# Ten loads moved from SyncE's DMA queue to GpSimd's: the residual for its turn, the output matrix and its bias

## The chip, the cores and the metric

The kernel runs on one core of one Trainium2 chip. Its time is the device time of one execution in microseconds (us); a lower time is better. A core has five engines that work side by side, each through its own list of instructions in order: PE (matrix multiplication), DVE (vector work), ACT (activation functions, copies), POOL (GpSimd) and SP (SyncE). A transfer between the large memory (HBM) and the on-chip memory is issued by one of the engines, as an instruction in its list, and then runs by itself on the core's 16 DMA engines. In this kernel SP does nothing but issue transfers (nearly all loads), and POOL issues nearly all stores. An issue instruction that must wait, for a buffer to be free or for data to be written, holds everything behind it in its engine's list.

## The reference, cut to what matters

Two layers of attention over a picture of 48 by 48 positions (N = 2304 tokens, 768 channels, 12 heads of 64), each on a group-normalised input, each added to the residual:

```
x = x + layer0(group_norm(x))      # qkv with a low-rank addition to q and v
x = x + layer1(group_norm(x))      # qkv with q scaled twice

layer(x):
    q, k, v = x @ qkv_w + qkv_b                    # 12 heads of 64
    s = q @ k.T * scale + rel_h[q, key row] + rel_w[q, key column]
    o = softmax(s) @ v
    return o @ proj_w + proj_b
```

All data is float32. The tables `rel_h` and `rel_w` depend on the query and on the row or the column of the key.

## The kernel before, in words

Each layer runs three stages: `project` (normalise, make k, v, q and the position terms, store them to HBM), attention (`attend_plain`), and `out_project` (the product with the output matrix, plus the residual).

**Attention.** The loop goes over six pairs of heads, and for each pair over five blocks of queries: four of 512 and one of 256. A block's 18 key tiles (`kt`) are done in two batches of nine. For a tile PE makes the scores of both heads (L954, `ps_sc`, three PSUM buffers), ACT takes their exponential (L981, `pt`), and DVE adds it to a running sum (L987, from the second tile of a block on). PE is always one batch of scores ahead of the products with v: in `catch_up` it runs, for the batch before, the products `ps_ov` and, for a block's second batch, first the denominators `ps_d` from the sum. DVE then takes their reciprocal (L1021) and multiplies (L1025), ACT adds the bias of v (L1026), and POOL stores the denominators' reciprocals (L1032, `f_rec`) and the block (L1030, `f_o`). At the end of a block's sum ACT and DVE split it in three bfloat16 parts (L996 to L999).

The exponentials are taken without subtracting the row's maximum; at the end `judge` looks at the stored reciprocals, and only if they are out of range is everything computed again by a slower way (`attend_shifted`). With these inputs that second run isn't taken, and all that follows is about the first.

**What SP loads in attention, in this order.** For each block, while the block before it is computed: two loads of q (L932) and 24 of the position terms (`rel`, L942 and L946). At the end of a pair, also the four loads of the next pair's keys (L899, `k`, two for each batch of tiles) and two of its values (L908, `v`). The keys have one set of buffers, so a load of keys waits until PE has used the last pair's keys of the same batch.

**What runs beside it.** After every block but the first, `next(beside, None)` runs one step of the generator `beside`. In layer 0 its steps are: load the output matrix's bias (`bt`, L1288, shown as `bproj`) and the output matrix (`w_all`, L1293, shown as `wproj`, 2304 KB), and then four additions on the matrix, one a step (L412). In layer 1, between the two loads, comes `turn`: for each of six pieces of the residual (`res`, channels by tokens, 1152 KB each, numbered 0 to 5) it loads the piece (L1223, `x_turned<-f_res`), adds the bias on ACT (L1226, six activations, three in each of two steps), transposes 32 by 32 blocks on DVE (L1231) and stores the piece by 24 small transfers issued by POOL (L1238, `f_res_tokens`, 48 KB each). All pieces, and then the output matrix, use the same single buffer (tag `"w"` in the pool `p3_w`, one buffer). So the load of the next piece, and the load of the matrix, can only be issued when the 24 stores of the piece before have been written.

**What sets the order.** A scheduler places the instructions of each engine ahead of time; `in_order` keeps those it names in the order in which the program gives them on their engine. Each queue has eight semaphores for its transfers, used in turn: an issue also waits for the transfer eight places before it in the same queue.

Of the kernel before, what the change touches and what calls it, by code (L numbers as in the profile page):

```python
# [18 lines left out]
P = 128  # L19
# [52 lines left out]
def compute(ctx: ExitStack, tc: tile.TileContext, x, layers, out, run, bad):  # L72


    nc = tc.nc
# [35 lines left out]
    def scratch(name, shape):  # L111
        name = f"{run}_{name}"
        return dram.tile(shape, F32, tag=name, name=name)
# [16 lines left out]
    with ExitStack() as hots:  # L130
# [4 lines left out]
        for i, (rows, pattern, shape) in enumerate(parts):  # L135
            t = hotp.tile([rows, *shape], F32, tag=f"h{i}", name=f"hot_{i}")
# [21 lines left out]
    def in_order(instruction):  # L158

        tc.keep_in_program_order(instruction)  # L160
# [4 lines left out]
    def load_transposed(xT, raw, res, weights, low_rank):  # L165


        with tc.tile_pool(name="ps_x", bufs=3, space=PSUM) as ps_x:
            loaded = [xT[b].rearrange("p t q -> p (t q)") for b in range(NQB)]
            loaded = [l.rearrange("p (j c) -> p j c", j=TPB) for l in loaded]  # L170
            for b in range(NQB):
                nc.sync.dma_start(loaded[b], x[ts(b, QB), :].rearrange("(j p) c -> p j c", p=P))
            weights.load(0)
            weights.begin()
            if not shifted:
                load_places()
            for b in range(NQB):
                if b == 2:
                    next(low_rank)
                for t in range(CT):  # L180
                    ps = ps_x.tile([P, QB], F32, tag="ps", name=f"psx_{b}_{t}")
                    for j in range(TPB):
                        in_order(nc.tensor.transpose(
                            ps[:, ts(j, P)], loaded[b][:, j, ts(t, P)], ident
                        ))
                    nc.scalar.copy(raw[b][:, t, :], ps)
                    nc.vector.bn_stats(stats[:, t, b, :], raw[b][:, t, :])

            weights.spread()
            for b in range(HB):  # L190
                for i in (b, b + HB):
                    in_order(nc.gpsimd.dma_start(res[i], raw[i]))

    def group_norm(xT, raw, gn, between, beside):


# [220 lines left out]
    def matrix_blocks(w, n):  # L417

        return {
            f"{j + 1}{i + 1}": w[:, i * HP : (i + 1) * HP, ts(j, n)]  # L420
            for i in range(2) for j in range(2)
        }
# [28 lines left out]
    def project(ly, li, xT, kv, weights, first, normalise):  # L451


        PARTS = range(1 if shifted else 2)
        PART = F32 if shifted else F32R
        qd, kd = (
            [[scratch(f"{x}{li}_{half}_{i}", [P, HP, N]) for i in PARTS] for half in range(2)]
            for x in "qk"
        )

        vd = scratch(f"v{li}", [N, C])
        rel_d = [
            [
                [scratch(f"r{li}_{a}_{half}_{i}", [2 * HG, HP, N]) for i in PARTS]
                for half in range(2)
            ]
            for a in range(2)
        ]
        project_kv(ly, li, xT, kv, weights, first, normalise, PARTS, PART, kd, vd)
        return qd, kd, vd, rel_d  # L470

    def third_of_k(weights, g):

        w, room = weights.take("k", g)
        s = room.rearrange("p (i t n) -> p i t n", i=3, t=HP)
        return sums_of_a(matrix_blocks(w, P), *(s[:, i] for i in range(3)))
# [739 lines left out]
    def turn(res, to, pool, bt):  # L1216


        for b in range(NQB):

            both = pool.tile([P, 2, CT, QB], F32, tag="w", name=f"x_turned_{b}")
            x, turned = both[:, 0], both[:, 1]
            in_order(nc.sync.dma_start(x, res[b]))  # L1223
            yield
            for t in range(CT):
                in_order(nc.scalar.activation(  # L1226
                    x[:, t], x[:, t], AF.Identity, bias=bt[:, t : t + 1]
                ))
                if t == HP - 1:
                    yield  # L1230
            in_order(nc.vector.transpose(  # L1231
                turned.rearrange("p t q -> p (t q)"), x.rearrange("p t q -> p (t q)")
            ))
            rows = to[ts(b, QB), :].rearrange("(f i) c -> i f c", i=32)
            for t in range(CT):
                for r in range(P // 32):
                    lo = t * P + r * 32
                    in_order(nc.gpsimd.dma_start(  # L1238
                        rows[:, :, lo : lo + 32],
                        turned[ts(r, 32), t].rearrange("p (f j) -> p f j", j=32),  # L1240
                    ))
# [19 lines left out]
    for li, ly in enumerate(layers):  # L1261
        last = li == len(layers) - 1
        with tc.tile_pool(name="p1_kv", bufs=1, **REUSE) as kv:
            raw = xT
            low_rank = weights.low_rank(kv)
            if li == 0:


                raw = [
                    kv.tile([P, 2, CT, QB], F32, tag=tag, name=f"raw_{tag}")  # L1270
                    for tag in ("t1", "t2", "vw")
                ]
                raw = [raw[b % HB][:, b // HB] for b in range(NQB)]
                load_transposed(xT, raw, residuals[0], weights, low_rank)
                first, k_steps = third_of_k(weights, 0)
            normalise = group_norm(xT, raw, gn, low_rank, k_steps)
            qd, kd, vd, rel_d = project(ly, li, xT, kv, weights, first, normalise)
        project_q(ly, li, xT, weights, qd, rel_d)
        es.close()
        od = [  # L1280
            scratch(f"o{li}_{lo}", [CT, P, min(OB, N - lo)]) for lo in range(0, N, OB)
        ]
        with tc.tile_pool(name="p3_w", bufs=1, **REUSE) as p3:
            bt = p3.tile([P, CT], F32, tag="bt", name="bproj")
            w = {}

            def beside(li=li, ly=ly, p3=p3, bt=bt, w=w):
                in_order(nc.sync.dma_start(bt, ly.proj_bt))  # L1288
                if li == 1:
                    yield from turn(residuals[1], res_tokens, p3, bt)  # L1290
                w_all = p3.tile([P, CT, C], F32, tag="w", name="wproj")
                s = p3.tile([P, 3, HP, HP * P], F32, tag="s", name="wproj_s")
                in_order(nc.sync.dma_start(w_all, ly.proj_w.rearrange("(t p) n -> p t n", p=P)))  # L1293
                factors, steps = sums_of_a(
                    matrix_blocks(w_all, HP * P), *(s[:, i] for i in range(3))
                )
                w.update(factors)
                yield
                yield from steps

            attend(li, qd, kd, vd, rel_d, od, beside())


            es = ExitStack()
            xT = None
            if last:
                p3_first = es.enter_context(
                    tc.tile_pool(name="p3_first", bufs=1, side="right", **REUSE)
                )

                y_2, y_1, *first_out, y_0 = (
                    p3_first.tile(shape, F32, tag=name, name=name)
                    for name, shape in (
                        ("y_1_2", [P, 2, C]), ("y_1_1", [P, 2, C]), ("oT_1_0", [P, CT, QB]),
                        ("oT_1_1", [P, CT, QB]), ("y_1_0", [P, 2, C]),
                    )
                )
                first_out += [y_0, y_1, y_2]
            else:
                xT, gn, weights = begin(1, es)  # L1320
                first_out = [xT[HB], xT[NQB - 1]]
            prepared = []

            def prepare(weights=weights):
                weights.begin()
                weights.spread()
                weights.load(0)
                prepared.extend(third_of_k(weights, 0))
                yield
                yield from prepared[1]  # L1330

            k_steps = prepare()
            out_project(
                li, od, w, bt, first_out, res_tokens if last else residuals[li], xT,
                None if last else residuals[li + 1], iter(()) if last else k_steps,
            )
            if not last:
                first, k_steps = prepared
# [56 lines left out]
```

## Time and profile before

| what | us |
|---|---|
| median of three runs | 3287.63 |
| lowest and highest run | 3285.56 and 3287.98 |
| the profiled execution's own time | 3286.01 |
| its span, from the first instruction to the last | 3284.0 |
| PE busy in the span | 3209.8 (98%) |
| DVE busy | 2111.7 (64%) |
| ACT busy | 1450.6 (44%) |
| POOL busy | 462.0 (14%) |
| granted clock of PE, mean over the span | 0.99 |
| attention of layer 0, first to last reciprocal (L1021) | 976.39 |
| attention of layer 1, the same | 1006.36 |

Of the profiled execution's 3286.01 us, 2.0 us lie outside its span. The numbers in the timeline are microseconds from the span's start. The two layers run the same attention on the same shapes, so the two last rows can be laid side by side, reciprocal by reciprocal: there are 30, one for each pair and block. The difference between two neighbouring starts is called a lap here. In the profile, "issue" is time in which an engine waited for nothing that the profile shows, SPq is SP's list of issues, and the granted clock of PE is 1.00 at full speed.

### The profile page before, as it was taken

The numbers are of one execution on the slowest core, as the hardware profiler recorded it, in microseconds if no ns is written. First come the engines' busy times: TensorE is split into PE (matmuls) and PEld (weight loads), VectorE is DVE, ScalarE is ACT, GpSimd is POOL, SyncE is SP. The second block draws the span as 40 slices with busy tenths as digits, with TensorE's granted clock in tenths as the row PEclk, the third lists the DMA queues.
The fourth block names the chain that finished last, engine by engine and source line by source line (L and its number), as shares of the span: only waits on it lengthen the run. The fifth ranks groups of instructions, "written<-read, shape, count | busy, mean of one in ns | idle before, by whom it ended". The sixth has DMA issues, their size and how long they took to land.

```text
span 3284.0 us, 50036 instructions
## 1 busy us (share of the span) xinstructions
PE 3209.8 (98%) x19600; PEld 1993.1 (61%) x19600; DVE 2111.7 (64%) x2281; ACT 1450.6 (44%) x1673; POOL 462.0 (14%) x845
## 2 busy tenths in 40 slices
PE   8999999999999999999989999998999989999998
PEld 5555666566656566656555566665665556656565
DVE  8432437777777777776774234676777767777764
ACT  3101336555555555553011024564665555555520
POOL 2144110000000000000012531102223200000000
PEclk9999999999999999999999999999999999999999
DMA  7333488353435262725234346756556463435251
GB/s 266 130 82 76 133 263 217 83 124 81 123 82 136 68 147 67 151 61 180 93 127 139 55 123 204 228 124 142 116 137 129 119 162 75 127 80 133 69 201 59
DMA packets 226148, 419.77 MB, mean 128 GB/s; under 512 B 43840, under 2 KB 111328, under 8 KB 222064
## 3 DMA queue, kind: packets, MB, share of 16 engines
q1 hardware_dynamic: 180432, 267.16, 32.5%
q0 software_dynamic: 45472, 149.32, 15.2%
q8 instruction: 158, 2.59, 0.4%
q14 instruction: 86, 0.70, 0.1%
HBM read 260.35 MB, written 155.97 MB: 127 GB/s over the span
## 4 chain that ended last, share of the span: by engine, by line
PE 89%; issue 3%; DVE 3%; DMA 2%; ACT 1%; POOL 1%; SPq 1%; DVEq 0%; POOLq 0%; ACTq 0%
PE ps_sc L954 34%; PE ps_ov L954 24%; PE ps_q L698 9%; PE ps_v L523 7%; PE psy L1186 7%; PE ps_k L523 4%; PE psr L637 1%; PE ps_d L954 1%; DVE sum L987 1%; PE psc L637 1%; DMA rel<-f_r 1%; DVE relw L392 1%; POOL f_k L567 1%; ACT pt L981 1%; ACT relw L391 0%
## 5 line engine op out<-in xcount | busy, mean ns | idle before, releaser
L987 DVE TENSOR_TENSOR sum<-sum,pt 128x1024 f32<-128x1024 f32 (+1 forms) x960 | 1070.9, 1116 | 187.4 <-ACT pt L981 96.7
L954 PE MATMUL ps_sc<-q,k 64*128 64x512 f32 (+1 forms) x8640 | 1087.1, 371 | 25.2 <-issue 11.8
L981 ACT ACTIVATE pt<-ps_sc 128x1024 f32<-128x1024 f32 (+1 forms) x1080 | 1010.3, 941 | 196.4 <-PE ps_sc L954 110.5
L954 PEld LDWEIGHTS ps_sc<-q,k 64*128 64x128 f32 x8640 | 781.7, 186 | 239.4 <-issue 69.0
L954 PE MATMUL ps_ov<-pt,v 128*64 128x512 f32 (+1 forms) x4320 | 857.7, 551 | 0.0
L954 PEld LDWEIGHTS ps_ov<-pt,v 128*64 128x64 f32 x4320 | 301.1, 137 | 497.6 <-issue 443.3
L954 PE MATMUL ps_sc<-rel,places 64*128 64x512 f32 (+1 forms) x2160 | 414.0, 371 | 1.6 <-DMA rel<-f_r 1.3
L698 PE MATMUL ps_q<-xT,w_q 128*128 128x384 f32 x864 | 285.3, 489 | 0.7 <-DVE v L587 0.7
L1032 POOL DMA_DIRECT2D f_rec<-rec x120 | 58.4, 491 | 1612.1 <-DVE rec L1021 1612.1
L1026 ACT ACTIVATE o<-o,v_bias 128x512 f32<-128x512 f32 (+1 forms) x60 | 40.9, 682 | 450.4 <-DVE o L1025 450.4
L954 PEld LDWEIGHTS ps_sc<-rel,places 64*128 64x128 f32 x2160 | 211.8, 185 | 33.7 <-DMA rel<-f_r 1.6
L698 PEld LDWEIGHTS ps_q<-xT,w_q 128*128 128x128 f32 x864 | 163.1, 191 | 110.3 <-issue 2.6
L1021 DVE RECIPROCAL rec<-ps_d 128x512 f32<-128x512 f32 (+1 forms) x60 | 181.8, 3030 | 2.5 <-PE ps_d L954 2.5
L987 DVE TENSOR_TENSOR sum<-pt 128x1024 f32<-128x1024 f32 (+1 forms) x60 | 67.0, 1117 | 146.5 <-ACT pt L981 146.5
L601 POOL DMA_DIRECT2D f_v<-v x288 | 137.3, 485 | 106.5 <-DVE v L587 94.8
L523 PE MATMUL ps_k<-xt,w_k 128*128 128x384 f32 x432 | 143.4, 487 | 3.6 <-DVE xt L427 2.6
L704 DVE TENSOR_SCALAR x_q<-ps_q,bt 128x384 f32<-128x384 f32 x72 | 44.3, 617 | 159.4 <-PE ps_q L698 159.4
L996 ACT CAST sum<-sum 128x1024 bf16<-128x1024 f32 (+1 forms) x60 | 57.6, 960 | 169.3 <-DVE sum L987 169.3
L523 PE MATMUL ps_k<-xT,w_k 128*128 128x384 f32 x324 | 115.7, 511 | 4.7 <-DVE xT L249 4.6
L523 PEld LDWEIGHTS ps_k<-xt,w_k 128*128 128x128 f32 x432 | 81.5, 190 | 63.0 <-PE ps_k L523 3.0
L999 DVE TENSOR_TENSOR sum<-sum,sum 128x1024 bf16<-128x1024 f32 (+1 forms) x60 | 67.1, 1119 | 61.6 <-ACT sum L998 61.6
L997 DVE TENSOR_TENSOR sum<-sum,sum 128x1024 f32<-128x1024 f32 (+1 forms) x60 | 67.1, 1118 | 61.6 <-ACT sum L996 61.6
(180 smaller groups left out, 2464.3 us busy)
## 6 DMA issues: line engine op xcount, KB each, us to landing
rel<-f_r SPq DMA_DIRECT2D x1152, 96.0 KB, 4.2
f_k<-xs POOLq DMA_DIRECT2D x72, 384.0 KB, 2.9
f_q<-xs_q POOLq DMA_DIRECT2D x48, 576.0 KB, 3.8
k<-f_k SPq DMA_DIRECT2D x48, 576.0 KB, 5.1
q<-f_q SPq DMA_DIRECT2D x96, 256.0 KB, 3.3
f_r<-relh POOLq DMA_DIRECT2D x48, 432.0 KB, 5.0
f_r<-relw POOLq DMA_DIRECT2D x8, 2592.0 KB, 18.0
f_v<-v POOLq DMA_DIRECT2D x288, 48.0 KB, 2.0
```

The costliest lines, as they stand in the source:

```text
L523: nc.tensor.matmul(ps, lhsT=x, rhs=y, start=(t == 0), stop=(t == HP - 1))
L601: nc.gpsimd.dma_start(vd[to : to + KG, :], v[ts(r, KG), k])
L637: nc.tensor.matmul(ps[:, i, :, :], lhsT=weights.tables[a][:, 2 * s : 2 * (s + HG)], rhs=lines_of(l0 + i), start=True, stop=True,)
L698: nc.tensor.matmul(ps, lhsT=w[:, t, ts(pr, P)], rhs=xT[b][:, t, :], start=(t == 0), stop=(t == CT - 1),)
L954: in_order(nc.tensor.matmul(*args, **kwargs))
L981: nc.scalar.activation(pt, ps[:, :, 0 : self.n], AF.Exp)
L987: nc.vector.tensor_add(self.sum, self.first if kt == 1 else self.sum, pt)
L997: nc.vector.tensor_sub(self.sum, self.sum, hi)
L999: nc.vector.tensor_sub(lo, self.sum, mid)
L1021: nc.vector.reciprocal(self.rec, ps)
L1032: nc.gpsimd.dma_start(recs[li][2 * self.pair + r : 2 * self.pair + r + 1, to], self.rec[r * HD : r * HD + 1, :],)
L1186: nc.tensor.matmul(ps, lhsT=x, rhs=y, start=(t == 0), stop=(t == HP - 1))
```

## The change

Three calls change their engine, from `nc.sync` (SP) to `nc.gpsimd` (POOL). On the run that is executed these are ten transfers: the bias of each layer (two), the output matrix of each layer (two), and the six pieces of the residual in layer 1. What is loaded, where to, and the buffers stay as they are.

```
@@ turn
-            in_order(nc.sync.dma_start(x, res[b]))
+            in_order(nc.gpsimd.dma_start(x, res[b]))
@@ beside
-                in_order(nc.sync.dma_start(bt, ly.proj_bt))
+                in_order(nc.gpsimd.dma_start(bt, ly.proj_bt))
                 if li == 1:
                     yield from turn(residuals[1], res_tokens, p3, bt)
                 w_all = p3.tile([P, CT, C], F32, tag="w", name="wproj")
                 s = p3.tile([P, 3, HP, HP * P], F32, tag="s", name="wproj_s")
-                in_order(nc.sync.dma_start(w_all, ly.proj_w.rearrange("(t p) n -> p t n", p=P)))
+                in_order(nc.gpsimd.dma_start(w_all, ly.proj_w.rearrange("(t p) n -> p t n", p=P)))
```

Because POOL keeps the calls named by `in_order` in the order of the program, each moved load stands in POOL's list behind the 24 stores that free its buffer. In that list the load of piece 1 comes behind a store of `o` and two of the reciprocals, those of pieces 2, 3 and 5 and of the output matrix behind the stores of one block as well, and that of piece 4 directly behind the 24 stores. The lists of PE, DVE and ACT are the same in both kernels on the run that is executed; SP's list lacks the ten loads, and in two places two loads of q stand three places later among the loads of `rel`.

## The prediction

> **What bounds the kernel now.** I read the page first: PE is busy for 98% of the span, so time can only be won where PE stands still or runs at a lower clock. The laps between the reciprocals (L1021) show where. Layer 1's 30 laps follow layer 0's within 0.1 us almost everywhere, and sum to 1006.36 - 976.39 = 29.97 us more. Two laps hold nearly all of it:
>
> ```profile
> 2254.99 3.35 DVE L1021 RECIPROCAL rec<-ps_d 128x512 f32<-128x512 f32 x1
> 2296.31 1.75 DVE L1021 RECIPROCAL rec<-ps_d 128x256 f32<-128x256 f32 x1
> ...
> 2609.85 3.35 DVE L1021 RECIPROCAL rec<-ps_d 128x512 f32<-128x512 f32 x1
> 2651.47 1.75 DVE L1021 RECIPROCAL rec<-ps_d 128x256 f32<-128x256 f32 x1
> ```
>
> These laps are 41.32 and 41.62 us; the same lap at an undisturbed end of a pair (2962.52 to 2990.98) is 28.46. The excesses are 12.9 and 13.2 us, 26 together. They lie at the ends of pairs 0 and 2 of layer 1; call them gap A and gap B. The timeline shows what PE waits for:
>
> ```profile
> 2243.24 0.30 SPq L946 DMA_DIRECT2D rel<-f_r  x1
> 2266.04 0.34 SPq L1223 DMA_DIRECT2D x_turned<-f_res  x1
> 2272.35 1.62 ACT L1226 ACTIVATE x_turned<-x_turned,bproj 128x384 f32<-128x384 f32 x3 [1.77 <-DMA x_turned<-f_res]
> 2275.08 2.51 SPq L899 DMA_DIRECT2D k<-f_k  x4
> 2280.81 1.22 PE L954 MATMUL ps_sc<-q,k 64*128 64x512 f32 x4 [11.19 <-DMA k<-f_k]
> ...
> 2622.12 0.40 SPq L1293 DMA_DIRECT2D wproj<-in_proj_w_dram  x1
> 2631.15 1.36 DVE L412 TENSOR_TENSOR wproj_s<-wproj 128x1152 f32<-128x1152 f32 x1 [4.99 <-DMA wproj<-in_proj_w_dram]
> 2631.68 1.91 SPq L899 DMA_DIRECT2D k<-f_k  x4
> ```
>
> SP issues nothing from 2243 to 2266, because the load of piece 1 waits for piece 0's stores. The next pair's keys stand behind it and go out at 2275; PE, done at 2269.6, waits for them until 2280.8. In gap B the matrix does the same (PE idle 2624.2 to 2636.0). SP's waits name the cause, and an undisturbed end of a pair shows keys issued in time:
>
> ```profile
> SPq L1223 <- DMA f_res_tokens<-x_turned: 109.9, 14, 21.4
> SPq L1293 <- DMA f_res_tokens<-x_turned: 21.4, 4, 17.0
> ...
> 2959.68 14.95 SPq L899 DMA_DIRECT2D k<-f_k  x4
> 2978.12 1.19 PE L954 MATMUL ps_sc<-q,k 64*128 64x512 f32 x8
> ```
>
> The windows show that a gap costs more than its length: PE's clock falls during it and is still at half when work returns (columns: us, busy of PE, PEld, DVE, ACT, POOL with counts, clock, DMA share, GB/s):
>
> ```profile
> 2270.00:2281.00 11.00, 0.19 (x2) 0.23 (x4) 0.69 (x1) 2.20 (x4) 0.00 (x0) 0.62 1.06 223
> 2283.00:2285.00 2.00, 2.00 (x14) 1.53 (x12) 0.00 (x0) 1.02 (x1) 0.00 (x0) 0.50 1.06 360
> 2285.00:2287.00 2.00, 2.00 (x16) 1.58 (x14) 0.00 (x0) 0.87 (x1) 0.00 (x0) 0.69 1.15 325
> ```
>
> Full clock for 24% of the first window means it fell about 3 us into the gap; 38% of the last puts its return at 2286.2. So 5.4 us ran at half clock, 2.7 us of lost work.
>
> **The change part by part.**
>
> *Off SP.* Ten issues go: 6 x 0.34, 2 x 0.43 and 2 x 0.36 us, 3.6 in all, plus 131 us of holding. The rest of SP's order matters only at gaps A and B; elsewhere PE was fully busy through 20 us holds, because loads run a block ahead. At A the keys' first half is free when PE has passed tile 8 of the last block (about 2251) and the second at about 2265.3; both go as at 2959 to 2975, in time. I take the wait for keys as gone at A and B.
>
> *On to POOL.* The six pieces have the shape of L1214's stores on POOL (0.53 us each); the matrices are nearest to L630's (0.72), the biases to L1032's (0.49). That is 5.6 us of POOL, which is busy 14% of the span. Queued behind a waiting load are `f_rec` and `f_o`; their buffers are double and needed again a block (18 to 37 us) later, while the load waits about 2 us for the last store to land. I cost that at nothing; were it longer than a block, DVE would stop at L1025.
>
> *Pieces 2 to 5.* They issue right after stores that POOL issues anyway, at 2339.0, 2414.0, 2476 and 2547.3, against 2338.8, 2412.0, 2475.7 and 2545.4 on SP. With 0.5 us of issue and 6.5 to land they arrive 5 to 8 us before their activations (2353.8, 2428.8, 2488.0, 2562.4). Piece 0 has 50 us. Cost nothing; the cover is those 5 us at piece 4. Layer 0's loads have over 40 us before L412.
>
> *Piece 1, gap A.* The stores still land at 2266.0, so the load can't start earlier than on SP. With 0.53 of issue and 6.5 of landing (L1223's median) it is there at 2273.1. Bounds for the landing, from 1152 KB rows of POOL: 4.5 (fastest L1214) and 15.9 (six stores at once); I take SP's, the same transfer. ACT then does 1.62 of activations and 1.02 of exponential, to 2275.8. PE may run three score tiles ahead, 3 x 1.15 = 3.45 us, to about 2273.2: stall 2.6 us. The end of pair 1 supports the method: activations ending at 2456.55 plus 1.02 give 2457.57, where the fourth tile started at 2457.50 after a wait of 0.38. Gain at A: 12.9 - 2.6 = 10.3. At the bounds: stall 0.6, or 12.0 plus 2.7 of clock, which is no gain at all.
>
> *Matrix, gap B.* Now DVE is late next. Released at 2622.1, 0.7 of issue, 9.0 to land: 2631.8. The keys and `rel` loads, no longer held, now run beside it; I add 0.7, as k moves 576 KB a load at the same time: 2632.5. L412 ends at 2633.9. Undisturbed, the first sum starts 3.67 us after the products (2981.86 against 2978.19), here 2627.9: DVE is 6.0 us late. That passes through o (L1025) to ACT (L1026), which stands before the second batch's exponentials. There PE has 3.45 - 1.59 - 1.02 = 0.84 us to spare (scores at 2993.00, exponentials at 2994.59). Stall 5.2 us. In both gaps the clock fell about 3 us in (A above, B at 0.76 of the window from 2625 to 2630), so add 2.7: 7.9. Gain at B: 13.2 - 7.9 = 5.3. Bounds for the landing: 9.0 without company (stall 4.5) and 18.0 (`f_r<-relw`, 2592 KB on POOL, two at once), which would leave a stall of 13.5 and no gain.
>
> The Trainium skill, in "TensorE: Matmul & The Clock Gate", section "HAM oscillation — how this bites in real kernels", sets the limit at idle gaps of about 3.4 us. By that rule too a 5.2 us stall pays for a cold clock and one of 2.6 us doesn't, and the sum stays; the trace agrees with its falls at 3.0 and 3.4 us.
>
> Sum: 10.3 + 5.3 = 15.6 us off the profiled execution's 3286.0: 3270.4. The median of the runs is 1.6 above that execution: 3272.0.
>
> **The rivals.**
>
> *Only one gap closes.* The loads land late, because SP's queue, no longer held, competes for the same DMA engines (share above 1.0 in the gaps' windows). For: x and second-half keys now go out within 1 us of each other. Against: together they are 2.3 MB, some 6 us at the 407 GB/s of the window from 2281 to 2283. Three us later at both: A 5.6 + 2.7, B 8.2 + 2.7; gain 7: 3280.
>
> *Both close nearly.* Loads land at their fast bounds and the clock stays up at B: stalls of 0.6 to 2 and 4.5; gain 20 to 21: 3267.
>
> *No change.* The gaps aren't SP's holds but the transfers themselves: 3287.6. Against: keys landed 5 us after issue and were issued 13 us later than at 2959. The Trainium skill, in "DMA: Bandwidth & Descriptors", section "Issuing engines are not separate DMA queues", says that issuing from several engines saves only the sequencer's time, usually small. By that rule this rival would hold; the trace disagrees as far as a wait in the list counts, since SP issued nothing for 23 us.
>
> *Slower: POOL's stores slip.* Until now SP was held during most bursts of 24 stores; now `rel` loads run beside them. POOL has eight places in flight at a pitch of 0.615 us, so a landing over 4.9 us (now 2.0, at most 4.1) stretches the burst. At 9.8 us the pitch doubles: 14.6 becomes 29 us, pieces 2 to 5 come 14 us later against 5 to 8 us of cover, and ACT holds PE some 6 us at each, plus clock: 4 x 8.7 = 35, and A and B stay as they are: 3322. It decides above about 7 us of landing, where the slip passes the cover. Against: in most blocks SP's 24 loads end (0.47 us each, 11 us) about when the burst begins.
>
> **How the numbers follow.** One gap smaller than computed or computed right, 3268 to 3276: 0.55, my forecast 3272. Both nearly closed, 3263 to 3268: 0.13. Only one closes, 3276 to 3283: 0.17. No change: 0.06. Slower: 0.09. Low 3264 and high 3283 leave out about 2 in 10. A measurement tells apart about 0.2%, 6.6 us: faster means below 3281.0, slower above 3294.2. Faster: 0.55 + 0.13 + 0.17, less a little of the last, 0.84; same 0.07; slower 0.09.
>
> **What would show it.** Right: L1223 and L1293 on POOL; SP's waits for `f_res_tokens` gone; at A keys issued before PE needs them, PE idle 2 to 3 us on ACT; at B L412 still waiting for `wproj`, L1026 late by some 6 us, one stall of PE on ACT. Laps: 31 at A, 36 at B, the others unchanged. Wrong: stores of `f_res_tokens` at a pitch above 0.62 us, loads of x over 8 us, ACT waiting for x inside a block, or a long wait for keys still there.

## The result, and the profile after

| | before | after |
|---|---|---|
| median, us | 3286.48 | 3278.51 |
| lowest and highest, us | 3283.94 and 3291.18 (14 runs) | 3271.01 and 3281.92 (14 runs) |
| the profiled execution's own time, us | 3286.01 | 3272.56 |
| its span, us | 3284.0 | 3270.8 |
| attention of layer 1, first to last reciprocal, us | 1006.36 | 993.35 |
| POOL busy, us | 462.0 | 468.4 |

The ratio of the times is 0.9973, with a 95% interval of 0.9965 to 0.9981: 8.0 us faster. The 13.2 us between the two profiled executions lie in layer 1's attention (13.0 us); the profiled execution of after is one of its quicker ones, 6 us below the median.

The laps at gap A and gap B show the gain. These are the reciprocals in the timeline of after that answer to those shown of before:

```profile
2256.45 3.35 DVE L1021 RECIPROCAL rec<-ps_d 128x512 f32<-128x512 f32 x1
2289.13 1.75 DVE L1021 RECIPROCAL rec<-ps_d 128x256 f32<-128x256 f32 x1
...
2603.04 3.35 DVE L1021 RECIPROCAL rec<-ps_d 128x512 f32<-128x512 f32 x1
2639.20 1.75 DVE L1021 RECIPROCAL rec<-ps_d 128x256 f32<-128x256 f32 x1
```

Gap A's lap fell from 41.32 to 32.68 us, gap B's from 41.62 to 36.16. The lap behind each became 0.3 and 0.6 us longer; the others moved by 0.4 us at most, most of them by less than 0.1. The timeline of after (start, duration, engine, line; in brackets the wait before it and what ended it) shows what stands in the gaps now:

```profile
2253.68 13.82 SPq L899 DMA_DIRECT2D k<-f_k  x4
2257.05 9.72 POOL L1238 DMA_DIRECT2D f_res_tokens<-x_turned  x16 [1.47 <-DMA f_res_tokens<-x_turned]
2268.79 0.57 POOL L1223 DMA_DIRECT2D x_turned<-f_res  x1 [0.47 <-issue]
2276.23 1.62 ACT L1226 ACTIVATE x_turned<-x_turned,bproj 128x384 f32<-128x384 f32 x3 [4.21 <-DMA x_turned<-f_res]
2278.82 2.07 PE L954 MATMUL ps_sc<-q,k 64*128 64x512 f32 x8 [4.07 <-ACT pt L981]
...
2598.70 16.04 SPq L899 DMA_DIRECT2D k<-f_k  x4
2616.35 0.90 POOL L1293 DMA_DIRECT2D wproj<-in_proj_w_dram  x1 [1.97 <-DMA f_res_tokens<-x_turned]
2628.81 1.36 DVE L412 TENSOR_TENSOR wproj_s<-wproj 128x1152 f32<-128x1152 f32 x1 [9.46 <-DMA wproj<-in_proj_w_dram]
2642.39 0.51 ACT L1026 ACTIVATE o<-o,v_bias 128x256 f32<-128x256 f32 x1 [13.29 <-DVE o L1025]
2643.86 2.08 PE L954 MATMUL ps_sc<-q,k 64*128 64x512 f32 x8 [7.88 <-ACT pt L981]
```

SP now issues the keys while PE still works (the four loads begin at 2253.68 and 2598.70), and PE waits for keys no longer. At A, ACT waits 4.2 us for piece 1 and PE 4.1 us for ACT. At B the chain is one link longer: DVE waits 9.5 us for the matrix, ACT stands at L1026 until DVE has come to it, and PE waits 7.9 us. These are the stalls that the prediction put in the place of the old ones, and both are longer than it said. The windows of after (us, busy of PE, PEld, DVE, ACT, POOL with counts, granted clock, DMA share, GB/s) show that both cost clock:

```profile
2278.00:2280.00 2.00, 1.18 (x6) 0.99 (x8) 0.29 (x1) 2.00 (x3) 0.00 (x0) 0.65 1.11 242
2280.00:2282.00 2.00, 2.00 (x14) 1.51 (x12) 1.90 (x2) 1.17 (x2) 0.00 (x0) 0.50 0.58 114
2282.00:2284.00 2.00, 2.00 (x20) 1.68 (x18) 1.48 (x2) 1.47 (x2) 0.00 (x0) 1.00 0.57 165
...
2643.00:2646.00 3.00, 2.14 (x10) 1.76 (x12) 2.05 (x2) 2.64 (x3) 0.59 (x1) 0.50 1.14 145
```

### The profile page after: what moved, and what is told of

It is laid out like the page before. It is cut to its first block, busy times and chain, and to the rows that moved or that the text cites. A ratio compares the mean times of both kernels' runs of the same rounds, so it can differ in the third digit from the quotient of the medians.

```text
span 3270.8 us, 50009 instructions
## 1 busy us (share of the span) xinstructions
PE 3209.8 (98%) x19600; PEld 1995.9 (61%) x19600; DVE 2112.6 (65%) x2281; ACT 1450.0 (44%) x1673; POOL 468.4 (14%) x855
## 5 line engine op out<-in xcount | busy, mean ns | idle before, releaser
L1026 ACT ACTIVATE o<-o,v_bias 128x512 f32<-128x512 f32 (+1 forms) x60 | 40.9, 681 | 459.2 <-DVE o L1025 453.6
```

## The experiments

The theory: time is lost wherever a load stands in a list behind stores that have only just been issued, whatever engine issues it, and somebody works for that load at once. The change lets the keys past, but leaves ACT and DVE waiting for the same late transfers. Rivals: that the choice of the engine itself is what pays or costs, and that the transfers get in each other's way on the DMA engines. In all runs "before" is the kernel before, run beside the others on the same chip; its median was 3286.67 us with the first four kernels and 3287.16 with the four after them.

### The change again, and its two halves

**again** is the changed kernel, with no line edited.

> The changed kernel once more, for another profiled execution: its first one took 3272.56 us, but the median of its runs is 3278.51. Theory (the loads' landing decides): the laps outside gaps A and B repeat within 0.4 us, and what differs between executions lies in the two gaps, where PE stalls on ACT behind a load of x (4.1 us the first time) and behind the matrix (7.9 us). An execution near the median shows 3 to 8 us more there, in a later landing or a colder clock. Rival (the spread lies elsewhere, for example in the stages outside attention): the two gaps repeat within 1 us and other laps differ.

Measured: 3278.94 us (3271.22 to 3289.32), ratio 0.9975 (0.9967 to 0.9984): the same gain. Its profiled execution (3274.53 us) has laps of 33.26 at A and 40.41 at B: A repeats, B does not. At B the matrix took 14.8 us to land instead of 12.4, and PE's stall was 12.1 us instead of 7.9. The theory was only half met: layer 1's attention is 4.9 us longer than in the first profile, but the whole execution only 2.0, so executions differ outside the two gaps too.

**x_only** moves the pieces of x alone:

```
 turn:    -  in_order(nc.sync.dma_start(x, res[b]))
          +  in_order(nc.gpsimd.dma_start(x, res[b]))
 beside:     in_order(nc.sync.dma_start(w_all, ...))      # as before
```

> Only the six loads of x are issued by GpSimd; the matrix and the bias stay on SyncE. Theory: gap A as in the changed kernel (lap about 32.7 us against 41.3), gap B as before (lap about 41.6, keys issued behind the matrix). 4 to 9 us faster than before. Rival (the matrix brings most of it): within 2 us of before.

**w_only** moves the matrix alone:

```
 turn:       in_order(nc.sync.dma_start(x, res[b]))       # as before
 beside:  -  in_order(nc.sync.dma_start(w_all, ...))
          +  in_order(nc.gpsimd.dma_start(w_all, ...))
```

> Only the output matrix is issued by GpSimd; x and the bias stay on SyncE. Theory: gap A as before (lap about 41.3 us), gap B as in the changed kernel (lap 36 to 39 against 41.6, DVE waiting 9 us or more for the matrix). 1 to 6 us faster than before. Rival (x brings all of it): no difference, or slower, where the wait of DVE costs as much as the wait for the keys did.

Measured: x_only 3277.65 us, ratio 0.9967 (0.9954 to 0.998); w_only 3286.21 us, ratio 0.9995 (0.9985 to 1.0004). The whole gain comes from x, and moving the matrix brings none that can be told from nothing. The timeline of x_only, PE at A and then gap B:

```profile
2277.68 2.08 PE L954 MATMUL ps_sc<-q,k 64*128 64x512 f32 x8 [4.15 <-ACT pt L981]
...
2615.57 0.40 SPq L1293 DMA_DIRECT2D wproj<-in_proj_w_dram  x1
2618.61 7.37 SPq L899 DMA_DIRECT2D k<-f_k  x4
2629.25 2.56 PE L954 MATMUL ps_sc<-q,k 64*128 64x512 f32 x8 [11.97 <-DMA k<-f_k]
```

A is as in the changed kernel (lap 33.45) and B as before (41.77). The timeline of w_only at gap B:

```profile
2607.75 15.79 SPq L899 DMA_DIRECT2D k<-f_k  x4
2627.80 0.90 POOL L1293 DMA_DIRECT2D wproj<-in_proj_w_dram  x1 [3.53 <-PE ps_sc L954]
2644.05 1.36 DVE L412 TENSOR_TENSOR wproj_s<-wproj 128x1152 f32<-128x1152 f32 x1 [15.69 <-DMA wproj<-in_proj_w_dram]
2659.10 2.08 PE L954 MATMUL ps_sc<-q,k 64*128 64x512 f32 x8 [14.11 <-ACT pt L981]
```

The keys go out in time, and yet the lap is 42.38 us: a wait of 12 us for keys has become one of 14.1 us on DVE and ACT. Here the matrix took 16.2 us to land, so this run takes the keys' wait away and makes the matrix later at once.

### Issue the loads a step later, on either engine

**late_sp** is the kernel before, all loads on SP, with one step more between a piece's 24 stores and the next load:

```
 turn:       (24 stores)
          +  yield
```

> The kernel before with one more step of the generator between a piece's stores and the next load (three steps a piece, not two), so that every load comes a block later, when the stores have long landed; all loads stay on SyncE, and the same work is done. Theory (what costs is a wait in a list, on whichever engine): SyncE holds nothing, ACT and DVE don't wait for loads, laps at A and B 28.5 to 30.5 us, 22 to 27 us faster than before: 3260 to 3265. Rival (GpSimd as issuer is what helps): within 3 us of before. Second rival (the loads themselves take the time, by competing for the DMA engines): at most the gain of the change, 8 us.

**late_pool** is the changed kernel, loads on POOL, with the same line.

> The changed kernel with one step more after each piece's 24 stores, so that every load is issued a block after the stores that free its buffer, now from GpSimd. Theory (what costs time is a load that waits in a list for stores just issued, not the engine that issues it): no load waits, both gaps are gone on this engine too, 3253 to 3260 us, within 3 us of the same step with the loads on SyncE (3256); the laps at the old gaps 27 to 30 us. The matrix may again take 12 to 16 us to land, against 9 to 12 on SyncE, but has a block of 37 us to do it in, since the sums follow one step later. Rival (GpSimd's queue is itself worse, or slows the stores): 3262 us or more. Rival (it is better in itself): below 3252 us.

Measured: late_sp 3256.25 us (3254.56 to 3260.5), ratio 0.9909 (0.9894 to 0.9923), 30 us faster than before and somewhat more than expected; late_pool 3255.99 us, ratio 0.9909 (0.9893 to 0.9924). The engine makes no difference once no load stands in front of work that is due; both are 22 us faster than the changed kernel. The rival that the engine itself matters is out. The view of waits (what waited, for what: us in total, times, longest) of late_sp shows that SP is still held:

```profile
SPq L1223 <- DMA f_res_tokens<-x_turned: 52.5, 10, 14.9
```

but no longer in front of keys. Its timeline at the place of gap A, and at the matrix:

```profile
2254.68 3.35 DVE L1021 RECIPROCAL rec<-ps_d 128x512 f32<-128x512 f32 x1
2281.99 1.75 DVE L1021 RECIPROCAL rec<-ps_d 128x256 f32<-128x256 f32 x1
...
2780.11 1.02 SPq L1294 DMA_DIRECT2D wproj<-in_proj_w_dram  x1
2785.01 0.42 SPq L942 DMA_DIRECT2D rel<-f_r  x1
2792.36 0.30 SPq L946 DMA_DIRECT2D rel<-f_r  x1
```

The lap at A is 27.31 us, without a stall. The last two lines are neighbours in SP's list and matter further down. In late_pool the matrix at the same place took 18.8 us to land instead of 12.2, and nobody waited for it:

```profile
2782.66 0.90 POOL L1294 DMA_DIRECT2D wproj<-in_proj_w_dram  x1 [4.22 <-DMA f_res_tokens<-x_turned]
2813.93 1.35 DVE L412 TENSOR_TENSOR wproj_s<-wproj 128x1152 f32<-128x1152 f32 x1
```

### One step between a load and those who need it

These three leave the place of the wait in the lists alone and give the waiting engine a block's time. **w_step** is the changed kernel, **w_step_sp** the kernel before, each with this in `beside`:

```
             w.update(factors)
          +  if li == 1:
          +      yield
             yield
```

> The changed kernel with one step more in layer 1 between the load of the output matrix and its first sum on VectorE. Theory (what is left of gap B is VectorE waiting for the matrix, and through L1025 and L1026 ScalarE and TensorE): the lap at B comes down from 36 to 40 us to 28.5 to 30, the one at A stays at 32.5 to 33.5; 7 to 11 us less than the changed kernel, 3267 to 3272 us. The matrix still takes 12 to 16 us from issue to landing, but nobody waits. Rival (what is left of gap B is contention of the transfers, of keys and matrix for the same DMA engines): the keys come late instead, the lap at B stays above 34 us, 3275 us or more.

> The kernel before, all loads on SyncE, with one step more in layer 1 between the load of the output matrix and its first sum. Theory (in the kernel before gap B is made by the keys that are held behind the matrix's load on SyncE, and VectorE's wait comes after it): the laps at A and B stay at 41 to 42 us, TensorE still waits about 12 us for the keys at B, 3283 to 3288 us. Rival (VectorE's wait for the matrix was the cause there too, and the keys no more than beside it): the lap at B comes down to below 35 us, 3279 us or less.

Measured: w_step 3263.98 us (3259.72 to 3270.91), ratio 0.9926 (0.9912 to 0.9939), 14.5 us below the changed kernel, more than expected. Its timeline at B:

```profile
2611.11 3.35 DVE L1021 RECIPROCAL rec<-ps_d 128x512 f32<-128x512 f32 x1
2626.59 0.90 POOL L1293 DMA_DIRECT2D wproj<-in_proj_w_dram  x1 [3.35 <-issue]
2638.28 1.75 DVE L1021 RECIPROCAL rec<-ps_d 128x256 f32<-128x256 f32 x1
2659.38 1.35 DVE L412 TENSOR_TENSOR wproj_s<-wproj 128x1152 f32<-128x1152 f32 x1
```

The lap is 27.17 us. The matrix landed 15.0 us after its issue, beside the keys' loads as in the changed kernel, and PE did not wait. So what was left of gap B was DVE's wait for the matrix and its way over ACT, not a late load of keys.

w_step_sp: 3287.98 us, ratio 1.0005 (0.9995 to 1.0014), as the theory had it. DVE's wait is gone there too (its first sum, at 2678.66, waits for nothing), but the keys are still held, and PE's wait at B is 13.2 us (the profile found no releaser for it; the keys' loads stand before it):

```profile
2627.21 0.40 SPq L1293 DMA_DIRECT2D wproj<-in_proj_w_dram  x1
2637.15 1.94 SPq L899 DMA_DIRECT2D k<-f_k  x4
2642.24 1.22 PE L954 MATMUL ps_sc<-q,k 64*128 64x512 f32 x4 [13.16 <-issue]
```

At B two waits lie one above the other. Taking away the keys' wait alone (w_only, where the matrix also lands later) brings nothing, taking away DVE's alone (w_step_sp) brings nothing, and taking away both (w_step) brings all of it.

**x_step** gives ACT the same for the pieces 1 to 5:

```
 turn:       in_order(nc.gpsimd.dma_start(x, res[b]))
          +  if b:
          +      yield
             yield
```

> The changed kernel with one step more between the load of each of the pieces 1 to 5 and its first activations, which puts the matrix at the end of pair 3 instead of pair 2, in the same place of that pair. Theory (what is left of gap A is ScalarE waiting for piece 1, 4.2 us): the lap at A comes down from 32.7 to 33.4 us to 28.5 to 30, and gap B appears unchanged, 36 to 41 us, four blocks later (between the reciprocals of the blocks 18 and 19); 3 to 6 us less than the changed kernel, 3273 to 3276 us. Rival (the load of 1152 KB itself slows the keys or TensorE): the lap at A stays above 31.5 us and the time within 2 us of the changed kernel.

Measured: 3276.58 us (3269.82 to 3279.41), ratio 0.9967 (0.9957 to 0.9977), not to be told from the changed kernel. Its timeline at A, and at the end of pair 3, where the matrix now is:

```profile
2257.74 3.35 DVE L1021 RECIPROCAL rec<-ps_d 128x512 f32<-128x512 f32 x1
2285.02 1.75 DVE L1021 RECIPROCAL rec<-ps_d 128x256 f32<-128x256 f32 x1
...
2784.51 0.90 POOL L1295 DMA_DIRECT2D wproj<-in_proj_w_dram  x1 [3.74 <-issue]
2803.73 1.36 DVE L412 TENSOR_TENSOR wproj_s<-wproj 128x1152 f32<-128x1152 f32 x1 [19.41 <-DMA wproj<-in_proj_w_dram]
2818.78 2.07 PE L954 MATMUL ps_sc<-q,k 64*128 64x512 f32 x8 [17.83 <-ACT pt L981]
```

A is settled: 27.28 us with PE standing nowhere, so ACT's wait for piece 1 was all that was left of it. But at its new place the matrix took 19.2 us to land, PE waited 17.8 us, and the lap is 46.11 us where 36 to 41 had been expected. What A gave, B took. That left one question: why this transfer takes 11 to 19 us from POOL, when it took 9.0 us twice from SP in the kernel before.

### The matrix's landing by itself

Both kernels change only layer 0 of the changed kernel, where nobody waits for the matrix: POOL clears the sums' buffer five or eleven times before it issues the load.

```
          +  if li == 0:
          +      for _ in range(5):      # w_quiet2: range(11)
          +          in_order(nc.gpsimd.memset(s..., 0.0))
             in_order(nc.gpsimd.dma_start(w_all, ...))
```

> The changed kernel, where in layer 0 alone GpSimd clears the buffer of the matrix's sums five times just before it issues the load of the output matrix, so that the load starts some 15 us later in the block, when SyncE has no loads of q and position terms under way. The result stays the same, since the buffer is written again. In the runs so far this load in layer 0 took 11.4 to 15.3 us from issue to landing on GpSimd, with SyncE's loads beside it, and 9.0 to 9.6 us on SyncE. Theory (it is slowed by SyncE's loads, which go on beside it; on SyncE the load eight places later waits for it, and so at most seven loads run beside it): 8 to 10 us. Rival (GpSimd's queue is itself slower for this transfer): 11 us or more. The load in layer 1 is not delayed and takes 12 to 16 us by both. The time of the kernel is that of the changed one, 3271 to 3283 us.

> The kernel of the run before, with eleven clearings of the sums' buffer in place of five (each took 3.03 us there). With five the load of the matrix in layer 0 went out at 566.0, in the middle of SyncE's next loads (561.6 to 581.5), so that run did not tell the two theories apart: the load had company and took 13.4 us. With eleven it goes out at about 584, where SyncE issues nothing until 599. Theory (it is slowed by the loads that SyncE issues beside it): 8 to 10 us from issue to landing. Rival (GpSimd's queue is itself slower for this transfer): 11 us or more. In layer 1, not delayed, 12 to 17 us by both.

Their times were 3275.38 and 3277.55 us (one run each; before beside them 3285.81 and 3287.8). w_quiet missed its aim: its load went out at 566.0, in the midst of SP's next loads, and took 13.4 us. In w_quiet2 it went out at 589.2, where SP issues nothing for 24 us. The timeline, and behind it the tile's line on landing in that window:

```profile
580.03 0.30 SPq L946 DMA_DIRECT2D rel<-f_r  x1
589.23 0.86 POOL L1296 DMA_DIRECT2D wproj<-in_proj_w_dram  x1
604.01 0.81 SPq L932 DMA_DIRECT2D q<-f_q  x2
```

```profile
DMA to landing us min/median/max: 8.9/8.9/8.9
```

Alone, POOL's load is as fast as SP's (in this one execution). So POOL's queue isn't slow; the company is. Over all runs with the matrix on POOL, the landing is mostly longer where SP issues more loads between the matrix's issue and its landing:

| loads issued by SP meanwhile | landing of the matrix, us |
|---|---|
| 0 | 8.9 |
| 3 and 5 | 11.4, 12.1 |
| 8 | 9.9, 12.4 |
| 10 | 14.8, 15.0 |
| 12 | 16.7 |
| 13 | 13.4, 14.2, 14.8 |
| 14 | 14.6, 15.3, 16.2, 18.8, 19.2 |

The table is rough. Loads already under way when the matrix starts aren't counted, and a long landing by itself leaves SP time for more loads, so the rows give no price for a load. In the first 8.9 us after the matrix's issue in layer 1 SP issued eight loads both in w_quiet2, where it landed after 9.9 us, and in x_step, where it landed after 19.2. What makes that difference stays open.

On SP the loads issued behind the matrix wait for it in the same queue. The view of transfers shows it (queue: packets, MB, share of the 16 engines' time): first the kernel before from 2622 to 2629 us, where the matrix was issued on SP at 2622.12 and seven `rel` loads behind it by 2625.99; then x_step from 2788 to 2800 us, where it had been issued on POOL:

```profile
q1 hardware_dynamic: 675, 2.07, 84.5%
...
q0 software_dynamic: 387, 2.32, 72.5%
q1 hardware_dynamic: 538, 0.84, 30.8%
```

Here q1 is SP's queue and q0 POOL's. The 675 packets are of 3072 bytes each, one row of the matrix; a row of `rel` has 2048 bytes, and none had moved yet. In x_step SP's loads, which stand in the other queue, move 0.84 MB beside the matrix's 2.32. So what shields the matrix on SP is the order within its queue. The eight places hold SP as well: in the kernel before it stood still from 2625.99 to 2631.14, and in late_sp, above, the eighth load (2792.36) went out only when the matrix had landed. But the seven loads let through did not move either, so no run here shows that this limit shortens the landing. And late_sp's 12.2 us came from what stood ahead of the matrix: from 2780.1 to 2783 us SP's queue moved 849 packets of about 0.5 KB, the size of the values' rows and not of the matrix's. The Trainium skill, in "DMA: Bandwidth & Descriptors", section "Queues, rings and completion order", says that each DMA engine takes turns between the queues that have work for it, a packet at a time. The lines of x_step agree with it as far as both queues move in the same 12 us; the turns of a single engine aren't seen in these traces.

## Why the prediction was right, and where it was off

The direction and the mechanism were right, and the median of 3278.5 lies in the range. The single number, 3272.0, was 6.5 us too low: the gain was computed as 15.6 us and measured as 8.0. The median lies where the prediction put its rival "Only one gap closes" (3276 to 3283 us, chance 0.17) and not in its own 3268 to 3276, and that rival's mechanism, loads that land late beside SP's, is what gap B shows. Step by step:

- **Off SP**: right. SP's waits for `f_res_tokens` are gone, the keys go out in time at both ends, and PE doesn't wait for them.
- **On to POOL**: right in kind. POOL's busy time rose by 6.4 us, not 5.6 (0.57 us for a piece, not 0.53; 0.88 for a matrix, not 0.72), and nobody waited for the stores queued behind a load.
- **Pieces 2 to 5**: right. ACT waited for one piece only, piece 1. The rival of slipping stores left a trace, though: the stores' median landing went from 2.0 to 2.4 us, and at A the burst lost 1.5 us to full places (the bracket at 2257.05). In w_quiet2, with layer 1's code unchanged, the waits around that burst reached 4.1 us (0.3, 1.2 and 2.6), ACT waited 7.9 us, and A's lap was 36.65. Single stores took up to 6.1 us to land there (6.2 in w_quiet2), more than the 4.9 at which the prediction let the burst stretch; the median stayed far from the 7 us at which this rival decides. A load over 8 us, another of the signs named for being wrong, appeared too (piece 0, 8.75 us), but nobody waited for it.
- **Piece 1, gap A**: mis-sized at the start of the load, which was taken from SP. It was issued 1.3 us later than computed (2268.79 against 2266.04, less the 1.46 us by which this whole execution runs later), mostly because those waits made the stores late; from issue to landing it took 7.1 us, as computed (0.53 + 6.5 = 7.0). PE's stall was 4.07 us and not 2.6, and it cost clock, which the prediction had put at nothing: x_step's undisturbed laps (27.28, then 33.31) leave 5.40 + 0.57 = 5.97 us, so 4.07 of stall and 1.9 of clock. The rule that the prediction cites from the Trainium skill, "TensorE: Matmul & The Clock Gate" (3.4 us), agrees for stalls of this length: in after, again and w_step the stalls at A are 4.07, 4.12 and 3.89 us, and the laps lose 5.97, 6.75 and 6.92 us. But the trace of w_step shows the clock falling after shorter waits: in layer 0 PE waited 1.50 us for `rel` and, half a microsecond of work later, 0.90 us more (until 536.60 and 537.96); its granted clock was 1.00 until 536.60, 0.63 in the next two microseconds and 0.50 from 538.60 to 542.00. So a stall of 2.6 us was not sure to be free either.
- **Matrix, gap B**: mis-sized at its first terms, the start and the landing. The matrix was issued 1.0 us later than computed (2616.35 against 2622.12, less the 6.81 us by which this execution is ahead here). Issue, landing and company were taken as 0.7 + 9.0 + 0.7 = 10.4 us; together they took 12.4 in the first profile and 14.8 in **again**. DVE was 9.0 us late instead of 6.0, the three microseconds of that rival, and PE stood 7.9 us instead of 5.2. That the lap nevertheless came out at the predicted 36 is luck, because other terms erred the other way: the undisturbed lap is 27.17 us here (w_step) and not the 28.46 read at another pair's end, and the clock cost 1.9 us, not 2.7: 36.16 - 27.17 + 34.06 - 33.31 = 9.74 = 7.88 + 1.86.
- **From one execution to the median**: the landing at B depends on how SP's loads happen to fall beside it, and varies. Four profiled executions with layer 1's attention as changed (after, again, w_quiet, w_quiet2) have B laps of 36.16, 40.41, 42.51 and 33.77 us, on average 38.2, and A laps of 32.68, 33.26, 32.93 and 36.65, on average 33.9. Against 36.3 and 31.0 as predicted that is 4.8 us more, and the laps behind the gaps take 1.4 more than before: 15.6 - 6.2 = 9.4 us of gain in this attention. That it is near the 8.0 between the medians is in part luck: the four took 3275.0 us on average, 11.0 less than the profiled execution of before and 3.5 less than the changed kernel's median. The prediction moved its sum to the median by 1.6 us, as the kernel before stands to its median, but there the gaps vary less: with the loads on SP the profiles show laps of 41.3 to 42.6 at A (before, w_only, w_step_sp) and 41.6 to 42.9 at B (before, x_only, w_step_sp). The rest lies within the spread of the executions (11 us), and its cause stays open.

The rival "No change" is out for gap A and was nearer the mark for the matrix than its chance of 0.06 said: by itself, moving it did nothing. The argument against it was right with other numbers: counted from the last full block's reciprocal, the keys of gap A went out 23 us (first half) and 10 us (second half) later than at 2959, not 13. The rule of the Trainium skill cited with it, in "DMA: Bandwidth & Descriptors", section "Issuing engines are not separate DMA queues", has two halves. That transfers from different engines share the DMA engines, the lines of x_step and the landing show; that a second issuing engine saves only the time of issuing doesn't hold where an issue waits: the ten issues took 3.6 us of SP, and moving them gained 8.0.

## What to carry to other kernels

When a load must wait for stores, moving it to the engine that issues the stores frees what stood behind it, but whoever needs the load still waits: ACT at A 1.8 us before and 4.2 after, DVE at B 5.0 and 9.5. Look for the next engine in line, and put time between the stores, the load and its use: one line (`yield`) gave 30 us here without moving anything, where the move gave 8. When a transfer leaves the queue in which the others stood behind it, price it by its new company too, not by its old duration alone.

## What the runs showed of the hardware that was not expected

- A 2304 KB load from HBM took 8.9 us from POOL with nothing of SP's beside it, and 18.8 and 19.2 us with 14 loads of 96 KB issued by SP meanwhile. These are 1.3 MB, little more than half of the matrix, and the landing more than doubled (what was already under way comes on top).
- The order of a queue protects a large transfer from the loads behind it: in the first 7 us after the matrix's issue on SP (before, from 2622 us) its queue moved 675 packets of 3072 bytes, all the matrix's, although seven more loads were issued. On SP the matrix landed in 8.9 to 9.6 us, and in 12.2 in late_sp, where it stood behind a load of values itself.
- One and the same order of instructions in layer 1 gave laps of 33.8 to 42.5 us at gap B in four executions. They follow the matrix's landing: 9.9 us with a lap of 33.77, 12.4 with 36.16, 14.8 with 40.41, 16.7 with 42.51.
- The granted clock fell to 0.50 after two waits of PE as short as 1.50 and 0.90 us (w_step, 535.1 to 538.0 us); after one of 1.42 us (again, until 533.55) it stayed at 1.00. In the long stalls it fell 2.0 us after PE had stopped (again, gap B) to 5.1 us after (w_only, gap B), so this case shows no fixed delay.
